# Cross-attention block on one core: the first nine steps and the last ones as lists of single-engine pieces

## The chip, the cores and the metric

The kernel runs on one core of one Trainium2 chip. The core has five engines with a queue of instructions each: PE (matmul; its weight loads are shown apart as PEld), DVE (vector), ACT (scalar and activation), POOL (GpSimd) and SP, which here only sends transfers. An engine works through its own queue in order and waits where an instruction needs another engine's result or a buffer that another still reads. The time is the device time in microseconds (us), the median of three runs.

## What is computed

A block of cross attention and a feed-forward net over x and ctx, both (128, 128, 256) in float32; 16 heads of 16, 1024 hidden units. Cut to what matters:

```python
q = (query @ Wq + bq).reshape(b, s, 16, 16).transpose(0, 2, 1, 3)   # k, v from ctx alike
scores = jnp.einsum('bhqd,bhkd->bhqk', q, k) / jnp.sqrt(16.0)
scores = jnp.where(j < i, scores, -1e30)          # a row sees the keys before it
attn = jax.nn.softmax(scores, axis=-1)
attn = attn.at[:, :, 0, :].set(0.0)
attn_out = einsum('bhqk,bhkd->bhqd', attn, v).transpose(0, 2, 1, 3).reshape(b, s, d) @ Wo + bo
x = layer_norm(query + attn_out, ln1_g, ln1_b)
ffn = jax.nn.relu(x @ W1 + b1) @ W2 + b2
out = layer_norm(x + ffn, ln2_g, ln2_b)
```

## The kernel before

The batch of 128 is done in 64 steps, p = 0 to 63, of two elements each. There is no scheduler: the order in which the program is written is the order in each engine's queue. Since the rows of a step are masked, its scores come in two halves: "hi" is the second half of the rows against all 128 keys (four PSUM banks, pss1_p_r), "lo" the first half against 64 keys (pss0_p_r).

One step goes as follows. The tokens get the bias of the output projection (`add_bo`, POOL, L265) and are transposed (`tokens`, DVE). PE projects keys, queries and values (`project`, `values`; pk, pq, pv), ACT copies them out as kT, qT and the two arrangements vz and vd of the values (L417, L427). PE makes the scores, DVE adds the mask (`mask`, L501) and takes the maximum (`maximum`), ACT the exponential, POOL the product with the reciprocal of the sums (`sums`, L540). The probabilities sm must then stand with keys on partitions: DVE transposes blocks of 32 (`turn`, L559, sm to tb) and 16 transfers (`bring`, L593, or `send` and `fetch` over memory) put the blocks at their places in pT. Steps 0 and 1 do it by PE instead (`turn_on_pe`, L608, into banks ptp, with a copy by ACT, L610). PE multiplies pT with the values (`weigh`, L625 and L635, pc), ACT copies that out (`context`, L647, cxT), PE makes the output projection (`attention_out`, L654, po), DVE adds the residual and takes statistics, ACT normalises (`norm1`), and x1 is transposed as x1T, by DVE and five transfers (`turn_x1`: x1t four times, then x1T). The net's two products are done by seven-product schemes in most steps (`Hidden`, L1155, with sums xS that POOL makes, and L1189 for the relus hT; `Second`, L1052, with sums hS by POOL, L1011 to L1017), in the first steps by plain products (`hidden`, L908; `second`). The second normalisation (`finish`, `norm2`, or the `_apart` forms with a bank pb) and `store` end the step, 2 to 5 steps after its scores.

PSUM has eight banks, b0 to b7, each a buffer that is rewritten only when its readers are done. In the first steps `bank()` deals out b4 to b7 in turn, by the order of the calls. Three arrays of 128 x 3072 a step (sm, tb, pT) share four wide buffers, in the order of the requests.

The steps are written in three ways. Steps 0 and 1 are inline (L1271 to L1333), steps 2 to 6 are functions (`third` L1352 to `sixth` L1529), steps 7 to 62 come from a table `order` of single pieces with a lag in steps (L1767), and the last step, with what is left of the ones ahead of it, is written out from L1807 on. In the first ways and the last, a call such as `maximum` or `sums` issues work on two or three engines at once.

Of the kernel before, what the change touches and what calls it, by code (L numbers as in the profile page):

```python
# [14 lines left out]
P = 128  # L15
# [5 lines left out]
def tile_cross_attention_block(  # L21
# [194 lines left out]
    turns = [0]  # L216

# [6 lines left out]

    def bank(name):
        turns[0] += 1
        return at_bank(4 + turns[0] % 4, name)
# [50 lines left out]
    def queries(p):  # L278
        st = states[p]
        st["qT"] = proj.tile([P, KC, TP], F32, tag="qT", name=f"qT_{p}")  # L280
        pq = project(wq, st["xT"], at_bank(4, f"pq_{p}") if p > 3 else bank(f"pq_{p}"))
        for m in range(KC):
            nc.scalar.activation(
                st["qT"][:, m, :], pq[:, m * TP : (m + 1) * TP], AF.Identity,
                bias=bqs_c[:, m : m + 1], scale=QSCALE,
            )
# [4 lines left out]
    def scale_wq():  # L291
        nc.scalar.activation(wq, wq, AF.Identity, bias=0.0, scale=QSCALE)
        nc.gpsimd.tensor_tensor(dq, bqs_c[:, 1:2], bqs_c[:, 0:1], ALU.subtract)

    def combine_wq():
# [83 lines left out]
    def keys(p):  # L379
        project_keys(p)  # L380
        copy_keys(p)

    def project_keys(p):
        st = states[p]
        st["kT"] = proj.tile([P, KC, 2, TP], F32, tag="kT", name=f"kT_{p}")
        st["pk"] = project(wk, st["cT"], at_bank(0, f"pk_{p}") if p > 3 else bank(f"pk_{p}"))

    def copy_keys(p, ms=range(KC), es=range(2)):
        st = states[p]
        pk = st["pk"]  # L390
        for m in ms:
# [15 lines left out]

    def values_out(p):
        spread_values(p)
        stack_values(p)  # L410
# [24 lines left out]

    def wide(name):
        return soft.tile([P, NS * (H + HH) * 32], F32, tag="wide", name=name, bufs=4)

    def room(p, hi):
# [4 lines left out]
        at = H * P if not hi else 0  # L444
        n = P if hi else HP
        st["sm", hi] = st["sm"][:, at : at + H * n].rearrange("p (h j) -> p h j", j=n)
        st["nmx", hi] = small.tile([P, H], F32, tag=f"nmx{hi}", name=f"nmx{hi}_{p}")

    def scores(p, hi):
# [18 lines left out]
        room(p, hi)  # L468

    def scores_both(p):  # L470

        st = states[p]
        for hi in range(2):
# [3 lines left out]
            room(p, hi)  # L477
        one, two = (0, 1), (2, 3)
# [17 lines left out]
    def mask(p, hi, rs):  # L496
# [3 lines left out]
        for r in rs:  # L500
            nc.vector.tensor_tensor(  # L501
                st["sm", hi][:, 4 * r : 4 * r + 4, :],
# [5 lines left out]
    def maximum(p, hi, part):  # L508
        st = states[p]
        n = P if hi else HP  # L510
        sm, nmx = st["sm", hi], st["nmx", hi]
        nc.vector.tensor_reduce(nmx[:, part], sm[:, part, :], AX.X, ALU.max, negate=True)
# [5 lines left out]
    def exponential(p, hi, part):  # L518
        sm = states[p]["sm", hi]
# [3 lines left out]

    def sums(p, hi, part):

        st = states[p]
        sm = st["sm", hi]
        n = sm.shape[2]
        rs = small.tile([P, H], F32, tag=f"rs{hi}", name=f"rs{hi}_{p}_{part.start}")
        if ("su", hi) in st:  # L530
            su, rs = st["su", hi][:, part], rs[:, part]
        else:
            su = small.tile([P, H], F32, tag=f"su{hi}", name=f"su{hi}_{p}_{part.start}")
            su, rs = su[:, part], rs[:, part]
            nc.vector.tensor_reduce(su, sm[:, part, :], AX.X, ALU.add)
        if ("rs", hi, part.start) in st:
            rs = st.pop(("rs", hi, part.start))
        else:
            nc.vector.reciprocal(rs, su)
# [4 lines left out]


# [7 lines left out]
    def turn(p, hi, t):  # L553

        st = states[p]
        if "tb" not in st:
# [4 lines left out]
            st["sm", hi].rearrange("p h j -> p (h j)")[:, t * 1024 : (t + 1) * 1024].rearrange(  # L561
# [35 lines left out]
    def turn_on_pe(p, hi, ts):  # L597

        st = states[p]
        sm = st["sm", hi].rearrange("p h j -> p (h j)")  # L600
# [3 lines left out]
        for t in ts:  # L604
            pt = bank(f"ptp{hi}_{p}_{t}")
            for i in range(4):
                at = (4 * t + i) * P
                nc.tensor.transpose(pt[:, i * P : (i + 1) * P], sm[:, at : at + P], ident)  # L608
            n = 4 * t if hi else H + 4 * t
            nc.scalar.copy(  # L610
                st["pT"][:, :, n : n + 4, :].rearrange("p i n a -> p n i a"),
                pt.rearrange("p (n i a) -> p n i a", i=NS, a=32),
            )
# [167 lines left out]
    def norm2_apart(p, at):  # L781
# [3 lines left out]
        ps = st["pb"] = at_bank(at, f"pb_{p}").rearrange("p (s d) -> p s d", s=2)  # L785
        for s in range(2):
# [4 lines left out]
    def finish_apart(p, parts=(0, 1)):  # L791
# [3 lines left out]
        if 1 in parts:  # L795
            nc.vector.tensor_tensor(t2, ps, be2_r[:, None, :].to_broadcast([P, 2, D]), ALU.add)
            store(p)
# [10 lines left out]
    def fold_norm1():  # L808


        ps = bank("ps_b1")
        n = DFF // NS
        for k in range(KC):
            for j in range(NS):
# [5 lines left out]
                )  # L820
        for j in range(NS):
            at = slice(32 * j, 32 * j + 1)
            nc.scalar.copy(b1s[at], ps[at, :n])
# [9 lines left out]
    def scale_w1():  # L833
        for k in range(KC):
# [4 lines left out]
    def fold_values():  # L839

        ps = bank("ps_bv")
# [5 lines left out]
        return ps  # L847

    def add_values(ps):
        nc.scalar.copy(bov_r, ps[:, :D])  # L850
# [29 lines left out]
    def turn_x1_on_pe(p):  # L880
        st = states[p]
        x1T = ffn.tile([P, NS, 4 * 32], F32, tag="x1T", name=f"x1T_{p}")
        st["x1T"] = x1T.rearrange("p i (s k a) -> p s i k a", s=2, k=KC)
        pt = transposed(st["x1"], f"ptn_{p}").rearrange(
            "p (k s i a) -> p k s i a", k=KC, s=2, i=NS
        )
        for k in range(KC):
            if p == 0:

                nc.scalar.activation(  # L890
                    st["x1T"][:, :, :, k, :], pt[:, k], AF.Identity,
                    bias=be1_c[:, k : k + 1], scale=g1_c[:, k : k + 1],
                )
            else:
                nc.scalar.copy(st["x1T"][:, :, :, k, :], pt[:, k])

    def hidden(p, fs, between=None, banks=(2, 3, 4, 0)):
        st = states[p]
        if fs[0] == 0:
            st["hT"] = ffn.tile([P, FC, TP], F32, tag="hT", name=f"hT_{p}", bufs=2)  # L900
        for f in fs[::2]:
            if p == 0:
                ph = bank(f"ph_{p}_{f}")
            else:
                ph = at_bank(banks[f // 2], f"ph_{p}_{f}")
            for i in range(2):
                for k in range(KC):
                    nc.tensor.matmul(  # L908
                        ph[:, i * TP : (i + 1) * TP].rearrange("p (s i a) -> p s i a", s=2, a=32),
                        w1[:, k, (f + i) * P : (f + i + 1) * P], st["x1T"][:, :, :, k, :],  # L910
                        start=(k == 0), stop=(k == KC - 1),
                    )
                    if p == 1:
                        empty(3 if f else 2)
            for i in range(2):
                nc.scalar.activation(
                    st["hT"][:, f + i, :], ph[:, i * TP : (i + 1) * TP], AF.Relu,
                    bias=(b1e_c if p else b1_c)[:, f + i : f + i + 1], scale=1.0,
                )
            if between:  # L920
                between(f)
# [23 lines left out]
    def mask_high(p, rs):  # L945
# [7 lines left out]
        for r in rs:  # L953
            nc.vector.tensor_reduce(
                st["nmx", 1][:, 4 * r : 4 * r + 4],
# [1099 lines left out]
```

## Time and profile before

| | us |
|---|---|
| median of three runs | 1487.75 (1486.59 to 1487.85) |
| the profiled execution's own time | 1487.3 |
| its span, first to last instruction | 1485.4 |
| PE busy | 1467.7 |
| POOL busy | 1390.1 |
| mean granted clock of PE | 0.999 |

How it is read: the span is what the trace covers, 1.9 us less than the execution's own time. Busy shares are means over stretches with different limits, so the windows, which give the busy time of each engine in a stretch, and the waits, which give what an engine waited for there, are needed beside them. In the rows of a trace, "out<-in" are the program's names for what is written and read, x is a count, and square brackets give the idle time before and what ended it. SPq and ACTq are the rows of transfers that SP and ACT send.

### The profile page before, as it was taken

To read this page: it belongs to the slowest core of one execution; us is meant where nothing else is said; L and a number is where in the kernel's file an instruction comes from. 1 tells how busy PE (TensorE), PEld (TensorE's weight loads), DVE (VectorE), ACT (ScalarE), POOL (GpSimd) and SP (SyncE) were. 2 spreads that over 40 slices of the span, in tenths; PEclk is the share of its full clock that TensorE was granted. 3 is DMA by queue.
4 is the path that set the end of the run, shared out by engine and by line. 5 is a ranking of instruction groups with operands and counts; after the bars stand their busy time and mean duration, and the time that the engine had idled before them with its cause. 6 is when DMAs were issued, how large, how long until landed. Compare 5 with 4: busy or idle time off the path is not lost.

```text
span 1485.4 us, 53956 instructions
## 1 busy us (share of the span) xinstructions
PE 1467.7 (99%) x19696; PEld 1380.1 (93%) x19696; DVE 1318.3 (89%) x2897; ACT 1323.7 (89%) x5279; POOL 1390.1 (94%) x1484
## 2 busy tenths in 40 slices
PE   8999999999999999999999999999999999999998
PEld 7788999999999999999999999999999999999988
DVE  7998899999999998999999989989989999999866
ACT  5657999999999999999999999999999999999863
POOL 6878899999999999999999999999999999999996
PEclk9999999999999999999999999999999999999999
DMA  8356556556666556566566566666565666564451
GB/s 202 84 112 146 137 137 144 140 140 143 148 138 150 137 136 154 141 138 143 143 135 160 138 136 141 144 140 153 139 142 134 147 141 151 139 146 120 113 163 57
DMA packets 417862, 206.20 MB, mean 139 GB/s; under 512 B 282432, under 2 KB 386112, under 8 KB 417600
## 3 DMA queue, kind: packets, MB, share of 16 engines
q1 hardware_dynamic: 415696, 201.70, 57.6%
q8 instruction: 158, 2.59, 0.8%
q10 hardware_dynamic: 1904, 1.06, 0.3%
q14 instruction: 104, 0.85, 0.2%
HBM read 71.84 MB, written 34.87 MB: 72 GB/s over the span
## 4 chain that ended last, share of the span: by engine, by line
PE 91%; POOL 3%; ACT 2%; DVE 2%; issue 1%; DMA 1%; POOLq 0%; ACTq 0%; DVEq 0%
PE phs L1155 25%; PE pX L1052 11%; PE py L1052 7%; PE pz L1052 7%; PE pv L403 7%; PE po L654 7%; PE pk L272 7%; PE pq L340 7%; PE pss L487 6%; PE pc L635 4%; PE pc L625 2%; ACT sm L985 1%; PE ph L908 1%; POOL sm L540 1%; PE pq L272 1%
## 5 line engine op out<-in xcount | busy, mean ns | idle before, releaser
L540 POOL TENSOR_TENSOR sm<-sm,rs 128x1024 f32<-128x1024 f32 x192 | 364.9, 1903 | 7.5 <-DVE rs L551 4.0
L985 ACT ACTIVATE sm<-pss,nmx 128x128 f32<-128x128 f32 x944 | 332.6, 399 | 8.0 <-issue 5.2
L985 ACT ACTIVATE sm<-sm,nmx 128x64 f32<-128x64 f32 x944 | 321.5, 360 | 2.4 <-DVE nmx L975 1.7
L1189 ACT ACTIVATE hT<-hT,b1e_c 128x256 f32<-128x256 f32 x480 | 216.0, 501 | 53.2 <-DVE hT L1180 53.2
L559 DVE STREAM_TRANSPOSE tb<-sm 128x1024 f32<-128x1024 f32 x186 | 227.3, 1225 | 1.3 <-POOL sm L540 1.1
L985 ACT ACTIVATION_READ_ACCUMULATOR sm<-pss,nmx 128x1 f32 x912 | 218.1, 239 | 0.0
L985 ACT ACTIVATION_READ_ACCUMULATOR sm<-sm,nmx 128x1 f32 x912 | 193.0, 212 | 0.0
L1155 PE MATMUL phs<-xS,w1t 128*128 128x128 f32 x1440 | 179.8, 275 | 0.7 <-POOL xS L1111 0.7
L1155 PEld LDWEIGHTS phs<-xS,w1t 128*128 128x128 f32 x1440 | 170.1, 192 | 0.9 <-POOL xS L1111 0.9
L968 DVE TENSOR_REDUCE nmx<-pss 128x4 f32<-128x512 f32 x224 | 152.8, 682 | 1.9
L393 ACT ACTIVATE kT<-pk,bkh,half 128x256 f32<-128x256 f32 x252 | 138.1, 557 | 4.1 <-PE pk L272 4.1
L501 DVE TENSOR_TENSOR sm<-pss,neg 128x256 f32<-128x256 f32 (+1 forms) x276 | 113.4, 437 | 17.8 <-PE pss L487 13.3
L1052 PE MATMUL pX<-wt,hS 128*128 128x128 f32 x960 | 127.1, 275 | 1.5 <-POOL hS L1015 1.3
L1155 PE MATMUL phs<-x1T,w 128*128 128x128 f32 x960 | 126.2, 275 | 1.0 <-DMA x1T<-x1t 0.8
L1155 PEld LDWEIGHTS phs<-x1T,w 128*128 128x128 f32 x960 | 120.7, 192 | 4.5 <-DMA x1T<-x1t 1.2
L654 PE MATMUL po<-wo,cxT 128*128 128x256 f32 x512 | 121.3, 380 | 0.8 <-ACT cxT L647 0.8
L403 PE MATMUL pv<-wv,cT 128*128 128x256 f32 x512 | 121.1, 379 | 0.0
L272 PE MATMUL pk<-cT,wk 128*128 128x256 f32 x504 | 119.4, 380 | 0.2 <-ACT sm L985 0.2
L1052 PEld LDWEIGHTS pX<-wt,hS 128*128 128x128 f32 x960 | 116.8, 192 | 1.9 <-POOL hS L1015 1.5
L403 PEld LDWEIGHTS pv<-wv,cT 128*128 128x128 f32 x512 | 97.1, 190 | 13.2
L654 PEld LDWEIGHTS po<-wo,cxT 128*128 128x128 f32 x512 | 92.7, 190 | 11.5 <-ACT cxT L647 1.4
L272 PEld LDWEIGHTS pk<-cT,wk 128*128 128x128 f32 x504 | 91.4, 190 | 10.7 <-ACT sm L985 0.4
(195 smaller groups left out, 4161.4 us busy)
## 6 DMA issues: line engine op xcount, KB each, us to landing
pT<-tb SPq DMA_DIRECT2D x968, 96.0 KB, 2.2
x1t<-tbx SPq DMA_DIRECT2D x252, 64.0 KB, 2.8
x1T<-x1t SPq DMA_DIRECT2D x63, 256.0 KB, 3.4
out_dram<-t SPq DMA_DIRECT2D x63, 256.0 KB, 4.4
xb<-in_x_dram SPq DMA_DIRECT2D x124, 128.0 KB, 3.2
cb<-in_ctx_dram SPq DMA_DIRECT2D x124, 128.0 KB, 3.4
x<-in_x_dram SPq DMA_DIRECT2D x31, 512.0 KB, 4.9
w<-in_L_xattn_W_dram SPq DMA_DIRECT2D x2, 1024.0 KB, 9.7
```

The lines of the kernel that those rows point to most:

```text
L272: nc.tensor.matmul(ps[:, m * TP : (m + 1) * TP], w[:, k, m * P : (m + 1) * P], src[:, k, :], start=(k == 0), stop=(k == KC - 1),)
L393: nc.scalar.activation(st["kT"][:, m, e, :], pk[:, m * TP : (m + 1) * TP], AF.Identity, bias=bkh[:, m, e : e + 1], scale=half[:, e : e + 1],)
L403: nc.tensor.matmul(pv[:, s * D : (s + 1) * D], st["cT"][:, k, s * P : (s + 1) * P], wv[:, k, :], start=(k == 0), stop=(k == KC - 1),)
L501: nc.vector.tensor_tensor(st["sm", hi][:, 4 * r : 4 * r + 4, :], st["sps", hi][r][:, : 4 * n].rearrange("p (n j) -> p n j", j=n), no[:, No ...
L540: nc.gpsimd.tensor_tensor(sm[:, part, :], sm[:, part, :], rs[:, :, None].to_broadcast([P, part.stop - part.start, n]), ALU.mult,)
L559: nc.vector.transpose(st["tb"][:, :, at : at + 256].rearrange("p j (n a) -> p n j a", a=32), st["sm", hi].rearrange("p h j -> p (h j)")[:, ...
L654: nc.tensor.matmul(po[:, s * D : (s + 1) * D], cxT[:, k, s, :], wo[:, k, :], start=(k == 0), stop=(k == KC - 1),)
L968: nc.vector.tensor_reduce(st["nmx", 1][:, 4 * r : 4 * r + 4], st["sps", 1][r].rearrange("p (n j) -> p n j", j=P), AX.X, ALU.max, negate=True,)
L985: nc.scalar.activation(sm[:, h, :], src, AF.Exp, bias=nmx[:, h : h + 1], scale=1.0, **({"accum_out": st["su", hi][:, h : h + 1]} if summed ...
L1052: nc.tensor.matmul(out, left(k), right(k), start=(first and k == 0), stop=(k == K - 1), skip_group_check=True,)
L1155: nc.tensor.matmul(ps[:, i * P : (i + 1) * P].rearrange("p (n a) -> p n a", a=32), left(i), right, start=(i == 0 and which not in self.ONT ...
L1189: nc.scalar.activation(self.hT[:, f], self.hT[:, f], AF.Relu, bias=b1e_c[:, f : f + 1], scale=1.0,)
```

## The change

The first nine slots (steps 0 to 8) and the last ones (from slot 61) are written as flat lists of pieces that use one engine each, in a newly chosen order. Between them the table's order stays, for slots 9 to 60. To that end the helpers are split: `maximum` (DVE) from `less` (POOL), `totals` and `reciprocal` (DVE) from `sums` (POOL), `turned` (PE) from `untile` (ACT), `project` from `keep_queries`, `x1_blocks` from `x1_untile`, `hidden` from `hidden_relu`; the last step's half into `last_products`, `last_sum`, `last_power`, `last_scale`, `last_shift` and `last_out`; `store` no longer stands in `finish_apart`. Banks of the first steps now come from a table by name (`HOMES`), wide buffers from a table `SOFT` for steps 0 to 6 and a rotation after that. Every instruction of before is there once, with its shape; the transfers of the second half of pT_2 are sent by SP, not by ACT.

```diff
     def bank(name):
-        turns[0] += 1
-        return at_bank(4 + turns[0] % 4, name)
+        return at_bank(HOMES[name], name)
...
     def wide(name):
-        return soft.tile([P, NS * (H + HH) * 32], F32, tag="wide", name=name, bufs=4)
+        kind, p = name.split("_")
+        turn_ = 3 * (int(p) - 7) + ("sm", "tb", "pT").index(kind)
+        at = SOFT[name] if name in SOFT else (2, 3, 1, 0)[turn_ % 4]
+        return soft.tile([P, NS * (H + HH) * 32], F32, tag=f"wide{at}", name=name)
...
+    def less(p, hi, part):
+        st = states[p]
         n = P if hi else HP
-        sm, nmx = st["sm", hi], st["nmx", hi]
-        nc.vector.tensor_reduce(nmx[:, part], sm[:, part, :], AX.X, ALU.max, negate=True)
+        sm, nmx = probabilities(p, hi), maxima(p, hi)
         nc.gpsimd.tensor_tensor(
...
     def steps(first, last):
...
+        for slot in range(first, last + 1):
+            for name, lag in order:
+                if 6 < slot - lag < NP - 1:
+                    ops[name](slot - lag)
...
-    turn_on_pe(0, 1, range(2))
-    add_values(ps_bv)
-    values_out(1)
-    turn_on_pe(0, 1, range(2, 4))
+    turned(0, 1, 0)
+    stack_values(1, (0,))
+    add_values()
...
-        hidden(0, range(3 * FC // 4, FC), lambda f: bring(p, nc.scalar, EVERY[8:]))
...
+    bring(2, nc.sync, EVERY[4:8])
+    bring(2, nc.sync, EVERY[12:16])
+    sums(3, 1, ONE)
+    bring(2, nc.sync, EVERY[8:12])
+    bring(2, nc.sync, EVERY[0:4])
...
-    steps(7, NP - 2)
+    steps(9, 60)
...
+    ops["relu0"](62)
+    context(61)
+    ops["n2b"](62)
...
+    last_sum(0)
+    last_products(1)
+    finish_apart(62, (0,))
+    finish_apart(61, (1,))
+    finish_apart(62, (1,))
+    store(61)
+    last_sum(1)
+    store(62)
+    store(58)
+    last_scale(0)
+    store(60)
+    store(59)
+    last_power(0)
+    last_scale(1)
+    last_shift(0)
+    last_power(1)
+    last_out(0)
+    last_shift(1)
+    last_out(1)
```

Three places show how the order moves. The first is ACT's queue where steps 0 and 1 meet: ptp are the transposed probabilities of step 0 (hi 0_0 to 0_3 and lo), pv the values of step 1. Before:

```order
L393 ACTIVATE kT_1_338<-pk_1_339,bkh_216,half_167 128x256 x4
L520 ACTIVATE sm_0_263<-sm_0_263 128x1024
L610 COPY pT_0_394<-ptp1_0_0_395 128x4x4x32
L610 COPY pT_0_394<-ptp1_0_1_401 128x4x4x32
L850 COPY bov_r_184<-ps_bv_359 128x256
L417 COPY vz1_178<-pv_1_354 128x8x2x16 x2
L427 COPY vd1_180<-pv_1_354 64x16x16 x2
L610 COPY pT_0_394<-ptp1_0_2_412 128x4x4x32
L610 COPY pT_0_394<-ptp1_0_3_418 128x4x4x32
```

And after:

```order
L421 COPY vz1_178<-pv_1_332 128x8x2x16
L540 ACTIVATE sm_0_273<-sm_0_273 128x1024
L431 COPY vd1_180<-pv_1_332 64x16x16
L867 COPY bov_r_184<-ps_bv_379 128x256
L431 COPY vd1_180<-pv_1_332 64x16x16
L627 COPY pT_0_402<-ptp1_0_0_383 128x4x4x32
L421 COPY vz1_178<-pv_1_332 128x8x2x16
L627 COPY pT_0_402<-ptp1_0_1_397 128x4x4x32
L627 COPY pT_0_402<-ptp1_0_3_416 128x4x4x32
```

Three of the four copies of pv_1 now stand ahead of the first pT copy, the last behind it. In both kernels ptp1_0_2 takes pv_1's bank.

The second place is ACT's queue where the last steps begin: hT_59 are the relus of step 59, cxT the context of step 61, which PE's next output projection reads. Before:

```order
L427 COPY vd0_176<-pv_62_22322 64x16x16
L1189 ACTIVATE hT_59_22328<-hT_59_22328,b1e_c_187 128x256
L770 ACTIVATE t2_57_21812<-t2_57_21812,nb_62_22359,sd_62_22358 128x256
L417 COPY vz0_174<-pv_62_22322 128x8x2x16
L1189 ACTIVATE hT_59_22328<-hT_59_22328,b1e_c_187 128x256 x7
L647 COPY cxT_182<-pc_61_22510 128x4x127
```

And after:

```order
L787 ACTIVATE t2_57_21643<-t2_57_21643,nb_62_21933,sd_62_21932 128x256
L421 COPY vz0_174<-pv_62_22101 128x8x2x16
L1190 ACTIVATE hT_59_22128<-hT_59_22128,b1e_c_187 128x256
L664 COPY cxT_182<-pc_61_22290 128x4x127
L787 ACTIVATE t2_57_21643<-t2_57_21643,nb_62_21933,sd_62_21932 128x256
L1190 ACTIVATE hT_59_22128<-hT_59_22128,b1e_c_187 128x256 x7
```

The copy to cxT moves ahead of seven relus and one half of a normalisation.

The third place is the end of DVE's queue: py_last_0 and _1 are the last step's two halves, pb_61 and pb_62 the second normalisations of steps 61 and 62. Before:

```order
L2009 TENSOR_TENSOR py_last_0_23367<-py_last_0_23367,t2_63_23251 128x256
L2011 BN_STATS bs_last_0_23377<-py_last_0_23367 128x6
L2012 BN_AGGR mv_last_23365<-bs_last_0_23377 128x2
L2015 SCALAR_TENSOR_TENSOR py_last_0_23367<-py_last_0_23367,mv_last_23365,g2_r_151 128x256
L794 TENSOR_TENSOR pb_62_23362<-pb_62_23362,g2_r_151 128x512
L796 TENSOR_TENSOR t2_62_23062<-pb_62_23362,be2_r_153 128x512
L2018 SCALAR_TENSOR_TENSOR t2_63_23251<-py_last_0_23367,sd_last_23366,be2_r_153 128x256
L2009 TENSOR_TENSOR py_last_1_23388<-py_last_1_23388,t2_63_23251 128x256
L2011 BN_STATS bs_last_1_23398<-py_last_1_23388 128x6
L2012 BN_AGGR mv_last_23365<-bs_last_1_23398 128x2
L2015 SCALAR_TENSOR_TENSOR py_last_1_23388<-py_last_1_23388,mv_last_23365,g2_r_151 128x256
L2018 SCALAR_TENSOR_TENSOR t2_63_23251<-py_last_1_23388,sd_last_23366,be2_r_153 128x256
```

And after:

```order
L1542 BN_AGGR mv_last_23191<-bs_last_0_23194 128x2
L811 TENSOR_TENSOR pb_62_23188<-pb_62_23188,g2_r_151 128x512
L813 TENSOR_TENSOR t2_61_22779<-pb_61_23148,be2_r_153 128x512
L813 TENSOR_TENSOR t2_62_22966<-pb_62_23188,be2_r_153 128x512
L1539 TENSOR_TENSOR py_last_1_23197<-py_last_1_23197,t2_63_23063 128x256
L1541 BN_STATS bs_last_1_23211<-py_last_1_23197 128x6
L1542 BN_AGGR mv_last_23191<-bs_last_1_23211 128x2
L1553 SCALAR_TENSOR_TENSOR py_last_0_23179<-py_last_0_23179,mv_last_23191,g2_r_151 128x256
L1553 SCALAR_TENSOR_TENSOR py_last_1_23197<-py_last_1_23197,mv_last_23191,g2_r_151 128x256
L1559 SCALAR_TENSOR_TENSOR t2_63_23063<-py_last_0_23179,sd_last_23192,be2_r_153 128x256
L1559 SCALAR_TENSOR_TENSOR t2_63_23063<-py_last_1_23197,sd_last_23192,be2_r_153 128x256
```

The scaling and the shift of the first half move behind the second half's statistics, and a piece of step 61 (pb_61) comes in between. On SP the five stores of steps 58 to 62 stand last in both kernels, ahead of the two of step 63; their order was 58, 60, 59, 61, 62 and is now 61, 62, 58, 60, 59. Step 61's store is then ready when its piece on DVE, shown above, is done.

More of the change, by code (lines that the diff above doesn't have):

```diff
@@ L898, in hidden, with hidden_relu @@
+    def hidden_relu(p, f):
         st = states[p]
-        if fs[0] == 0:
+        if "hT" not in st:
             st["hT"] = ffn.tile([P, FC, TP], F32, tag="hT", name=f"hT_{p}", bufs=2)
[L901 to L921, printed above, removed]
+        g = f // 2 * 2
+        nc.scalar.activation(
+            st["hT"][:, f, :], st["ph", g][:, (f - g) * TP : (f - g + 1) * TP], AF.Relu,
+            bias=(b1e_c if p else b1_c)[:, f : f + 1], scale=1.0,
+        )
@@ L1788, in step_tables @@
         return ops, order
+    ops, order = step_tables()
     def steps(first, last):
[L1791 to L1804 removed]
@@ new lines, in tile_cross_attention_block @@
+    less(3, 1, ONE)
+    mask(3, 1, (2,))
+    residual1(0, nc.gpsimd, (1,))
+    scores(3, 0)
+    maximum(3, 1, TWO)
+    second(0, 1)
+    norm1(1, (0,))
+    nc.gpsimd.tensor_tensor(b1e_c, b1e_c, b1_c, ALU.add)
+    less(3, 1, TWO)
+    block_x1(1)
+    mask(3, 0, (0,))
+    stack_values(3, (0,))
+    exponential(3, 1, ONE)
+    mask(3, 0, (2,))
+    scale_w1((0,))
+    mask(3, 0, (3,))
+    tokens(6, "x")
+    spread_values(3, (1,))
+    scale_w1((1,))
+    mask(3, 0, (1,))
+    maximum(3, 0, ALL)
@@ new lines, in tile_cross_attention_block @@
+    add_bo(63)
+    both_shifts(*later)
+    residual1(61, nc.gpsimd, (0,))
+    w60 = Second(60, banks=(1, 6, 4))
+    w60.run(2)
+    w60.run(4)
+    w60.run(1)
+    h61.run(4)
+    w60.run(5)
+    leave_x1(62)
+    fetch_x1(62)
+    w60.add(0)
+    w60.run(6)
+    h61.add5()
+    h61.add4()
+    w60.add(2)
+    w60.add(1)
+    h61.run(3)
+    weigh(63)
+    residual1(61, nc.gpsimd, (1,))
+    h61.add3()
+    w60.run(7)
+    combine_normed(62, (2,))
+    h61.relu(2)
+    combine_normed(62, (0,))
```

2015 lines of the change are left out of this document (1421 added, 594 removed), and 9 rows, old and new, of the table HOMES.

## The prediction

> **What bounds the kernel now.** I read the page first: the span, the engines' busy shares and the chain that ended last.
>
> ```profile
> span 1485.4 us, 53956 instructions
> PE 1467.7 (99%) x19696; PEld 1380.1 (93%) x19696; DVE 1318.3 (89%) x2897; ACT 1323.7 (89%) x5279; POOL 1390.1 (94%) x1484
> PE 91%; POOL 3%; ACT 2%; DVE 2%; issue 1%; DMA 1%; POOLq 0%; ACTq 0%; DVEq 0%
> ```
>
> PE is busy for 99% of the span, and 91% of the chain is its own work, so the matmuls set the time. The change keeps every matmul and every shape, and can only win time in which PE stands still or runs slowly. Where that is, the windows view tells: each row is a stretch, its length, the busy time of PE, PEld, DVE, ACT and POOL, the granted clock, the DMA share and GB/s.
>
> ```profile
> 20.00:30.00 10.00, 7.35 (x89) 5.52 (x95) 9.02 (x13) 7.21 (x16) 9.87 (x6) 0.88 0.95 270
> 40.00:172.00 132.00, 128.13 (x1575) 108.43 (x1556) 116.21 (x201) 93.08 (x274) 108.52 (x100) 1.00 0.52 118
> 172.00:1403.00 1231.00, 1231.00 (x16889) 1174.64 (x16887) 1119.12 (x2523) 1166.12 (x4833) 1187.48 (x1261) 1.00 0.60 141
> 1403.00:1486.00 83.00, 72.82 (x867) 68.26 (x865) 53.99 (x125) 42.11 (x133) 66.73 (x86) 0.99 0.39 109
> ...
> 24.00:28.00 4.00, 1.78 (x15) 1.58 (x14) 3.93 (x7) 3.09 (x9) 4.00 (x3) 0.96 1.12 347
> 28.00:31.00 3.00, 3.00 (x59) 2.34 (x61) 1.94 (x3) 2.50 (x4) 2.87 (x3) 0.50 0.69 110
> ```
>
> From 172 to 1403 us PE never stops. That stretch is steps 9 to 60, whose order is kept, so nothing is to be won there. The stops are at the two ends: 10.00 − 7.35 = 2.65 us in 20:30, 132.00 − 128.13 = 3.87 in 40:172, and 83.00 − 72.82 = 10.18 in the last stretch. There is also a slow piece: in 28:31 the clock is 0.50, so 3 us of PE time do 1.5 us of work, and in 24:28 it is 0.96, another 0.2: 1.7 us in all. The waits of PE name the releasers (total, times, longest), first for 0:172, then for 1403:1486; for 172:1403 the view is empty.
>
> ```profile
> PE ptp L608 <- issue: 2.2, 1, 2.2
> PE warm L1210 <- POOL ident masks.py:199: 1.5, 1, 1.5
> PE po L654 <- ACT cxT L647: 0.8, 1, 0.8
> PE pss L487 <- ACT hT L916: 0.8, 2, 0.6
> PE ph L908 <- ACT kT L393: 0.8, 1, 0.8
> PE phs L1155 <- POOL xS L1111: 0.7, 1, 0.7
> ...
> PE ph L908 <- DMA x1T<-x1t: 0.2, 1, 0.2
> ...
> PE pss L487 <- ACT cxT L647: 1.5, 1, 1.5
> PE pX L1052 <- POOL hS L1015: 1.3, 1, 1.3
> PE phs L1155 <- DMA x1T<-x1t: 0.8, 1, 0.8
> ```
>
> The end after the last matmul is the third place; here are PE's last work, DVE's and SP's last rows (start, duration, engine, line, operation).
>
> ```profile
> 1472.92 7.07 PE L2005 MATMUL py_last<-w,hT 128*128 128x256 f32 x32
> ...
> 1480.96 0.18 DVE L2012 BATCH_NORM_AGGREGATE mv_last<-bs_last 128x2 f32<-128x6 f32 x1
> 1481.18 0.49 DVE L2015 SCALAR_TENSOR_TENSOR py_last<-py_last,mv_last,g_r 128x256 f32<-128x256 f32 x1
> 1482.07 0.48 DVE L2018 SCALAR_TENSOR_TENSOR t<-py_last,sd_last,be_r 128x256 f32<-128x256 f32 x1 [0.40 <-POOL sd_last L2014]
> ...
> 1480.06 2.88 SPq L2019 DMA_DIRECT2D out_dram<-t  x2
> ```
>
> PE ends at 1472.92 + 7.07 = 1479.99. Of the 10.18 us in the last stretch 6.01 thus lie behind it, and 4.17 are waits. So at most 2.65 + 3.87 + 1.7 + 4.17 = 12.4 us can go ahead of the last matmul: a floor of 1487.3 − 12.4 = 1474.9 us for the profiled execution, 0.8% below it. A time that moves by less than 0.2% (3 us) I count as unchanged; that is about what a measurement of this kernel can tell.
>
> **The change part by part.** All sums are made against the profiled execution's own 1487.3 us (its span of 1485.4 and 1.9 around it), 0.45 below the median of 1487.75.
>
> *T1, the first bank wait.*
>
> ```profile
> 23.44 1.09 PE L608 MATMUL ptp<-ident,sm 128*128 128x128 f32 x8 [0.43 <-POOL sm L540]
> 26.75 1.51 PE L608 MATMUL ptp<-ident,sm 128*128 128x128 f32 x10 [2.22 <-issue]
> ...
> 24.13 1.07 ACT L610 COPY pT<-ptp 128x512 f32<-128x512 f32 x2 [1.51 <-PE ptp L608]
> 25.35 0.68 ACT L417 COPY vz<-pv 128x256 f32<-128x256 f32 x2
> 25.88 0.76 ACT L427 COPY vd<-pv 64x256 f32<-64x256 f32 x2
> ...
> 21.48 5.62 POOL L540 TENSOR_TENSOR sm<-sm,rs 128x1024 f32<-128x1024 f32 x3
> ...
> 24.07 1.22 DVE L501 TENSOR_TENSOR sm<-pss,neg 128x512 f32<-128x512 f32 x2
> ```
>
> The view says "issue", yet what PE waits for is the bank: the third transposed piece goes where pv_1 lies until ACT's four copies of it end at 26.64, and those stand behind two pT copies that wait for PE. After the change three of the four stand ahead of the first pT copy, one behind it: 24.13 + 0.55 for that copy + 0.35 for the last one and 0.1 to release give 25.1 instead of 26.75. The stop is 0.5 then. PE's 8 transposes from there take 0.9, to 26.0. Next it now does the low scores of step 1, whose banks DVE frees with four masks, at 24.07 + 4 × 0.61 = 26.5: a second stop of 0.6. The low transposes behind need POOL's third product, which ends at 21.48 + 5.62 = 27.10; the scores (0.6) cover that. With the 0.43 ahead of the first transposes, which POOL's product still sets (POOL is full here, 9.87 of 10), some 1.5 to 2.1 of the 2.65 are left: **−0.8** (bounds 0 and −2.2; I take the middle of what POOL's and DVE's rows allow).
>
> *T2, the slow clock.* The half clock comes right behind the 2.22 us stop. With that stop split into pieces of 0.4 to 0.6, no stretch is left in which PE is as empty as the 1.78 of 4.00 us of 24:28. The tail has a stop of 1.5 and one of 1.3 us, and its clock stays at 0.99 over 83 us. The new pieces are nearer to these than to 2.22: **−1.7** (bounds 0 and −1.7). [...]
>
> *T3, steps 2 to 8.* Here are 3.87 us of stops, 3.5 of them named above: ACT copies that stand behind an exponential or a relu (0.8, 0.8, 0.8), POOL's sums and small ones. The new lists put cxT, kT and the relus ahead of long ACT pieces and xS ahead of POOL's projections. Against this stands the SP queue: all 16 transfers of pT_2 go out there, where 8 went by ACT's.
>
> ```profile
> 58.73 1.22 DVE L559 STREAM_TRANSPOSE tb<-sm 128x1024 f32<-128x1024 f32 x1
> ...
> 62.46 4.46 ACTq L593 DMA_DIRECT2D pT<-tb  x7
> 64.03 5.99 SPq L593 DMA_DIRECT2D pT<-tb  x8
> ...
> 71.81 0.34 PE L625 MATMUL pc<-pT,vd 128*32 128x64 f32 x11
> ...
> pT<-tb SPq DMA_DIRECT2D x968, 96.0 KB, 2.2
> x1T<-x1t SPq DMA_DIRECT2D x63, 256.0 KB, 3.4
> ```
>
> Transfers start when tb's last third is done, now at 59.95. DVE then no longer has a residual between the thirds (0.6 earlier), and the step as a whole is 2.5 us ahead by T1 and T2: 56.9. Sixteen at 0.67 us (4.46 / 7 = 0.64, 5.99 / 8 = 0.75) take 10.7, and 2.2 to land: 69.8. PE wants pT_2 at 71.81 − 2.5 = 69.3, so it waits some 0.5 us; were the cover gone, it would be up to 8 × 0.67 = 5.4. I allow 0.7 more for the same in x1T_3 and pT_5, which stand behind transfers waiting for DVE. So 1.2 of the 3.87 stay: **−2.7** (bounds −3.9, and +2.2 with 5.4 in the place of 0.5). The banks and wide buffers of the tables are as many as before (4 and 4); I cost the new assignment at nothing beside T1, as PE's work between two uses of a bank is some us and covers the copy of 0.55.
>
> *T4, the last steps.* ACT and POOL in 1403:1412:
>
> ```profile
> 1404.32 2.90 ACT L1189 ACTIVATE hT<-hT,b1e_c 128x256 f32<-128x256 f32 x7
> 1411.73 1.27 POOL L1011 TENSOR_TENSOR hS<-hT 128x512 f32<-128x512 f32 x1
> ```
>
> cxT of step 61 stood behind these seven relus; now it stands ahead of six or seven of them, up to 2.8 us earlier, and the wait of 1.5 goes. The relus end 1.1 later (a copy of 0.56 and a normalising of 0.59), at 1408.3. POOL's first hS_59 stood behind seven 128x512 pieces; of these only three stand between the last product and it now, so it starts when the relus are done, some 3 us earlier, and the wait of 1.3 goes too. The x1T of step 61 is sent earlier, but still behind a pT block: I count 0.3 of its 0.8. Together **−3.1** (bounds 0 and −4.2).
>
> *T5, behind the last matmul.* DVE now does both last scalings after the second statistics, then both shifts: from 1481.14 four pieces at about 0.47 to 1483.0, where the last shift ended at 1482.55: +0.5. Three finishing pieces of 0.69 stand between the two halves' statistics and just fit before PE's end. And the five stores of 256 KB of steps 58 to 62, spread over 20 us before, are issued in the last 4, ahead of the two last ones: 1.3 MB at the 347 GB/s that 24:28 shows is 3.8 us from about 1479.8, done at 1483.6, while the last shift is sent at 1483.1; at the 109 GB/s of the last stretch it would be 12.0, done at 1491.8 where the span now ends at 1485.4. I take the first, being the stretch with many transfers queued at once, and 0.5 for sharing: **+1.0** (bounds +0.5 and +6.4).
>
> Sum: −0.8 − 1.7 − 2.7 − 3.1 + 1.0 = −7.3, so 1487.3 − 7.3 = 1480.0 for a profiled run and, with 0.45 to the median, **1480.5 us**.
>
> **The rivals.**
>
> [...]
>
> *The lead is not kept.* POOL is at 1187.48 of 1231.00 us in the steady stretch, 96%. If POOL, not PE, is ahead by less than the 5.2 us of T1 to T3, PE meets it again and waits at the first steps of the steady order; then only T4 and T5 remain, −2.1: 1485.6 (1487.75 − 2.1). For it: POOL's share. Against it: its slack of 43 us there, and POOL's own queue had gaps ahead of 172 (108.52 of 132 busy) that go with the reordering.
>
> *Slower: SP's queue as the bound of steps 2 to 8.* A step sends 16 pT, 4 x1t, one x1T and the loads through one queue; a transfer that waits for DVE holds all behind it, and PE wants x1T and pT at about the time when they land. If in each of these seven steps PE waits one landing (2.2 us) for it, it is 15.4 us: 1480.5 + 15.4 = 1495.9. It decides for slower from (7.3 + 3.0) / 7 = 1.5 us a step. For it: pT_2 comes out with no slack. Against it: 40:172 has a DMA share of 0.52, and only 0.2 us of a stop there is put down to a DMA now.
>
> *The order doesn't set the engines.* If what the new lists move is not what the waits hang on, every stop returns elsewhere: 1487.75, at most the end's +1.0.
>
> **How the numbers follow.** Forecast 0.60 (1476 to 1484), clock 0.14 (1482.2), lead lost 0.10 (1485.6), no effect 0.06 (1488), slower 0.10 (1496). The bounds 1484.8 and 1490.7 are 0.2% around the median. Faster: 0.60 + 0.14 + 0.01 from the lower side of the lead's loss = 0.75. Same: 0.09 + 0.06 = 0.15. Slower: 0.10. The range leaves out the slower case and the lower end of the sum's bounds (0.05): it goes from 1476.0, 1.1 above the floor, to 1488.5.
>
> **What would show it.** T1: ptp's second start near 25.1, after a stop of under 1 us. T2: 0.50 nowhere in 24:34. T3: PE busy over 130 of 132 in 40:172, and one stop at pc of step 2. T4: no stop over 0.5 us for cxT or hS behind 1395. T5: the time from PE's last end to the span's end 6.4 instead of 5.4 us. The forecast is wrong if PE has stops after 172, if SP's queue releases over 3 us of them ahead of it, or if the span behind the last matmul exceeds 9 us.

## The result and the profile after

| | before | after |
|---|---|---|
| median of four runs (us) | 1487.80 (1486.59 to 1488.63) | 1479.53 (1479.12 to 1480.06) |
| ratio, 95% interval | | 0.9945 (0.9928 to 0.9962) |
| profiled execution, its span (us) | 1487.3, 1485.4 | 1480.06, 1478.1 |

The changed kernel is 0.55% faster: 8.3 us by the medians, 7.3 by the two spans. Among the later runs two single executions, one of e_tail (7027.65 us) and one of b_copies (1509.18), lie far off the others of their kernels and do not enter the ratios. First the page of the changed kernel: span, engines, chain.

```profile
span 1478.1 us, 53969 instructions
PE 1464.9 (99%) x19696; PEld 1378.9 (93%) x19696; DVE 1316.4 (89%) x2897; ACT 1325.7 (90%) x5279; POOL 1389.8 (94%) x1484
PE 94%; POOL 1%; DVE 1%; DMA 1%; SPq 1%; issue 1%; ACT 0%; DVEq 0%; POOLq 0%
```

PE's share of the chain rises from 91 to 94%; the shares of POOL and ACT fall. The windows (length, busy time of PE, PEld, DVE, ACT, POOL, clock, DMA share, GB/s), with the stretch of steps 9 to 60 seven us earlier than before:

```profile
20.00:30.00 10.00, 8.99 (x116) 6.07 (x118) 9.90 (x17) 7.02 (x15) 10.00 (x6) 1.00 0.90 266
40.00:172.00 132.00, 130.41 (x1580) 113.77 (x1577) 119.45 (x210) 98.64 (x302) 113.86 (x107) 1.00 0.56 125
165.00:1396.00 1231.00, 1230.59 (x16880) 1174.01 (x16879) 1118.80 (x2522) 1164.66 (x4829) 1185.84 (x1260) 1.00 0.60 141
1396.00:1479.00 83.00, 73.61 (x876) 69.39 (x874) 54.41 (x126) 44.58 (x139) 67.24 (x87) 0.97 0.38 109
24.00:28.00 4.00, 3.25 (x55) 2.67 (x53) 3.96 (x8) 2.60 (x7) 4.00 (x3) 1.00 1.11 355
28.00:31.00 3.00, 3.00 (x94) 2.51 (x96) 3.00 (x7) 2.31 (x5) 3.00 (x3) 1.00 0.89 144
```

In 20:30 PE stands still for 1.01 us where it was 2.65, and the clock of 28:31 is 1.00 where it was 0.50. (The 0.97 of the 1396:1479 row comes from the 7 us behind PE's last work: 0.68 in 1472:1479, 1.00 in 1396:1472.) PE's waits, for 0:165, 165:1396 and 1396:1479:

```profile
PE pc L642 <- DMA pT<-tb: 1.1, 1, 1.1
PE ptp L619 <- POOL sm L557: 0.7, 1, 0.7
PE pc L642 <- DMA x1t<-tbx: 0.4, 1, 0.4
PE pss L476 <- ACT qT L294: 0.3, 1, 0.3
...
PE po L671 <- issue: 0.4, 1, 0.4
...
PE phs L1156 <- DMA x1T<-x1t: 1.9, 2, 1.6
PE pX L1064 <- POOL hS L1027: 0.2, 1, 0.2
```

The waits for ACT's copies (cxT, kT, hT) are gone from the first steps. What ends last there now are transfers, 1.1 and 0.4, the second at the products of step 2, and POOL's product, 0.7. In the last steps cxT is gone and hS is at 0.2, but a stop of 1.6 for x1T of step 60 is new. The end, from the timeline:

```profile
1469.84 1.89 PE L1528 MATMUL py_last<-w,hT 128*128 128x256 f32 x8
1471.04 2.73 SPq L816 DMA_DIRECT2D out_dram<-t  x5
1473.56 0.87 DVE L1559 SCALAR_TENSOR_TENSOR t<-py_last,sd_last,be_r 128x256 f32<-128x256 f32 x2
1474.06 1.19 SPq L1564 DMA_DIRECT2D out_dram<-t  x2
```

PE ends at 1471.73, and 6.4 us follow where 5.4 did. DVE's last shift ends at 1474.43, 2.7 us behind PE, where it was 2.6 (1482.55 − 1479.99), so nearly all of the 1.0 lies in the transfers: the five stores are sent in 2.73 us, right ahead of the two last ones.

To tell the first steps' share from that of the last, I read one landmark in each trace: the start of the same output projection in the steady stretch (that of step 58), and, at the head, of the scores of step 2. First the rows of before, then those of after.

```profile
39.36 0.90 PE L459 MATMUL pss<-kT,qT 32*64 32x256 f32 x24
...
1339.62 1.89 PE L654 MATMUL po<-wo,cxT 128*128 128x256 f32 x8
```

```profile
36.68 1.12 PE L476 MATMUL pss<-kT,qT 32*64 32x256 f32 x32
...
1333.66 1.89 PE L671 MATMUL po<-wo,cxT 128*128 128x256 f32 x8
```

At step 2's scores PE is 2.7 us ahead, in the steady stretch 6.0. The last matmul ends 8.3 ahead (1479.99 to 1471.73), so the last steps give 2.3; then 1.0 is lost behind it: 6.0 + 2.3 − 1.0 = 7.3.

### The profile page after: what moved, and what is told of

The parts are those of the page before. It is cut to its first block, busy times and chain, and to the rows that moved or that the text cites. A ratio compares the mean times of both kernels' runs of the same rounds, so it can differ in the third digit from the quotient of the medians.

```text
span 1478.1 us, 53969 instructions
## 1 busy us (share of the span) xinstructions
PE 1464.9 (99%) x19696; PEld 1378.9 (93%) x19696; DVE 1316.4 (89%) x2897; ACT 1325.7 (90%) x5279; POOL 1389.8 (94%) x1484
## 3 DMA queue, kind: packets, MB, share of 16 engines
q8 instruction: 158, 2.59, 0.8%
## 4 chain that ended last, share of the span: by engine, by line
PE 94%; POOL 1%; DVE 1%; DMA 1%; SPq 1%; issue 1%; ACT 0%; DVEq 0%; POOLq 0%
PE phs L1156 25%; PE pX L1064 11%; PE pk L281 7%; PE py L1064 7%; PE po L671 7%; PE pz L1064 7%; PE pv L411 7%; PE pq L351 7%; PE pss L502 6%; PE pc L652 4%; PE pc L642 2%; PE ph L917 1%; SPq L608 1%; DMA x1T<-x1t 1%; POOL sm L557 1%
## 5 line engine op out<-in xcount | busy, mean ns | idle before, releaser
L980 DVE TENSOR_REDUCE nmx<-pss 128x4 f32<-128x512 f32 x236 | 160.8, 683 | 1.9
```

Source lines behind the costliest of these rows:

```text
L980: nc.vector.tensor_reduce(maxima(p, 1)[:, 4 * r : 4 * r + 4], st["sps", 1][r].rearrange("p (n j) -> p n j", j=P), AX.X, ALU.max, negate=True,)
```

## The experiments

The table gives for each kernel the median, the ratio to the runs of before on its chip with its interval, and from its trace the lead of PE at that landmark against the first trace of before (late is positive), the further change of the last steps up to the last matmul, and the time behind it.

| kernel | median | ratio | lead, step 58 | last steps | behind |
|---|---|---|---|---|---|
| changed, first trace | 1479.53 | 0.9945 (0.9928–0.9962) | −6.0 | −2.3 | 6.4 |
| a_again | 1479.56 | 0.9950 (0.9938–0.9963) | −7.0 | −2.3 | 6.4 |
| e_head | 1479.70 | 0.9947 (0.9935–0.9959) | −7.8 | −0.4 | 5.4 |
| e_head2 | 1480.47 | 0.9954 (0.9942–0.9967) | −6.8 | −0.1 | 5.4 |
| e_tail | 1485.31 | 0.9986 (0.9977–0.9994) | −1.3 | −2.2 | 6.4 |
| b_copies | 1488.17 | 1.0003 (0.9994–1.0011) | −0.2 | −0.4 | 5.4 |
| b_fill | 1494.90 | 1.0046 (1.0033–1.0059) | +9.2 | −0.2 | 5.4 |
| b_shift | 1498.87 | 1.0079 (1.0065–1.0092) | +13.0 | +0.4 | 5.4 |
| b_ctx | 1487.51 | 1.0001 (0.9992–1.0009) | 0.0 | −0.2 | 5.4 |
| a_act | 1485.33 | 0.9984 (0.9975–0.9993) | −1.9 | −2.0 | 6.4 |
| a_end | 1480.37 | 0.9948 (0.9936–0.9960) | −7.2 | −0.1 | 5.4 |
| a_x1 | 1483.45 | 0.9968 (0.9956–0.9981) | −6.1 | 0.0 | 6.4 |
| a_best | 1477.41 | 0.9934 (0.9922–0.9946) | −6.6 | −3.4 | 5.4 |

### e_tail and e_head: one end of the program at a time

e_tail has the first steps (and the rules for banks and wide buffers) of before and the new list from slot 61 on; e_head the reverse.

```diff
-    scores(0, 1)
-    first_tokens(1, "c")
...
-    steps(9, 60)
+    third()
+    fourth()
+    fifth()
+    fall_in(5)
+    sixth(6)
+    steps(6, 60)
```

> The first nine steps in the order of before, the last steps in the new order. If the gain is the sum of separate places: the stops of the last steps shrink by about 2.3 us, the time behind the last matmul grows by about 1.0, so 1486.5 us against 1487.8 (-1.3). If the last steps gain only because the first ones hand them a lead: no change or slower, 1487.8 to 1489.

> The first nine steps in the new order, the last ones in the order of before. If the lead of the first steps is carried through the steady stretch: about -6.0 us, 1481.8. If POOL, or the steady order, takes the lead back and the gain sits in the last steps: 1486 to 1488, with stops of PE behind 172 us.

Both gain, so neither end hangs on the other. The lead of the first steps arrives unshortened at the landmark, and the last steps shrink by 2.2 us, pay 1.0 at the end, with or without that lead. Of e_tail's gain 1.3 us are not the last steps': its trace is that much ahead at the landmark, with the first steps of before, because its clock in 28:31 is 1.00 (see b_fill and b_shift). POOL does not take the lead back: the stretch 165:1396 has 1231.00 us of PE's work in e_head. e_head did better than its 1481.8: its lead was 7.8, not 6.0.

### a_again and e_head2: the changed kernel again, and beside it

> The changed kernel itself once more, as the measure for the two next ones: 1479.5 us within 1 us. If the 0.85 us by which PE's lead shrinks at slots 9 to 10 in its first trace belongs to the kernel, it is there again; if it is an accident of one execution, the lead in the steady stretch is larger this time (-6.8 or more against the kernel before).

> The first nine steps in the new order, the last ones in the order of before, beside the changed kernel on one chip. If the new order of the last steps adds something on top of the new first steps (its stops 2.3 us shorter, its end 1.0 us longer): about 1.3 us slower than the changed kernel, 1480.8. If it adds nothing on top: equal.

The second trace of the changed kernel has a lead of 7.0: the 0.85 us that the first one lost between the output projections of steps 8 and 9 belongs to that execution. Beside each other, the new last steps are worth 1480.47 − 1479.56 = 0.9 us, near the 1.3 expected; the two intervals overlap, so the runs alone don't show it, the traces (2.2 less stops, 1.0 more end) do.

### b_copies: only the first stop

```diff
-    turn_on_pe(0, 1, range(2))
     add_values(ps_bv)
     values_out(1)
+    turn_on_pe(0, 1, range(2))
```

> The kernel before with one thing moved: ACT's copy of the folded bias and its four copies of pv_1 stand ahead of the first two pT copies instead of behind them. If the first stop is the wait for pv_1's bank, it falls from 2.2 us to about 0.7; if the half clock comes from that stop, the clock is 1.00 in 28 to 31 us as well: -1.5 - 1.2 to 1.7, about -2.9 us in all (1484.9). [...]

A miss: no gain, although the stop did go (2.2 us for the bank before; 0.8 and 0.8 for POOL's product now) and the clock was 1.00. The scores of step 2 began 2.15 us earlier, at 37.21. Most of that is the clock: against e_tail, whose clock is 1.00 too and whose first stop is that of before, they begin 0.6 earlier (37.78 to 37.21). Then, at the products of step 2, the trace of this kernel has a stop that the kernel before does not have:

```profile
72.43 0.43 PE L625 MATMUL pc<-pT,vd 128*32 128x64 f32 x16 [2.92 <-DMA pT<-tb]
...
61.95 0.39 SPq L100 DMA_DIRECT2D x<-in_x_dram  x1
62.63 8.11 SPq L593 DMA_DIRECT2D pT<-tb  x8
```

SP sends its half of pT_2 from 62.63 to 70.74, in 8.11 us where the kernel before takes 5.99, and PE waits for it until 72.43. The earlier start by itself is not the cause. Right ahead of the eight stands a load of x, 512 KB, which the kernel before sends at 53.45. SP's waits for that load, first before, then in b_copies:

```profile
SPq L100 <- DMA xb<-in_x_dram: 1.1, 1, 1.1
...
SPq L100 <- DMA pT<-tb: 11.8, 1, 11.8
```

Here the load waits 11.8 us, until ACT's first transfer of pT_2 has landed at 61.89. In this kernel's trace the two carry the same semaphore number, 105; in the kernel before, the load shares its number, 104, with a transfer of xb that lands at 53.39. So moving ACT's copies also moved a load in among the transfers of pT_2, and those landed later: the median of ACT's eight is 3.7 us, where it was 2.4. That a lead can pass this place shows in e_tail, which comes to the products of step 2 at 70.17, 1.55 us ahead of the kernel before (71.72), without a stop there. The changed kernel sends all sixteen from 56.79 on, in 11.51 us, and there the stop is 0.4. What the first stop alone is worth at the end of the kernel is therefore not shown by this run.

### a_act: half of pT_2 by ACT's queue again

```diff
-    bring(2, nc.sync, EVERY[12:16])
+    bring(2, nc.scalar, EVERY[12:16])
...
-    bring(2, nc.sync, EVERY[8:12])
+    bring(2, nc.scalar, EVERY[8:12])
```

> The changed kernel with half of pT_2's transfers on ACT's queue again. If one queue for all sixteen costs PE the wait of 0.4 us at the products of step 2, that wait goes (-0.4 at most). If instead ACT, which is held about 5 us by sending them, delays its exponentials of step 3, the lead of the first steps shrinks: +0.5 to +3 us, with new stops of PE between 70 and 110 us.

5.8 us slower than the changed kernel, more than either theory gave. ACT comes to these transfers late, behind its exponentials:

```profile
72.90 0.32 PE L642 MATMUL pc<-pT,vd 128*32 128x64 f32 x8 [3.37 <-DMA pT<-tb]
...
65.68 1.23 ACTq L608 DMA_DIRECT2D pT<-tb  x2
```

SP's half is out by 61.6, ACT's begins at 65.68, and PE stops for 3.4 us; in the 3.5 us behind the stop the clock is 0.61, which adds to the loss. So in the new order, at this place of ACT's queue, the eight transfers cost most of the first steps' gain, and sending them by SP, which I had put down as a risk, saves it. An earlier place on ACT, such as the kernel before has (from 61.82 on), was not tried.

### b_fill and b_shift: the clock, and something else

b_fill gives PE work in the first stop; b_shift puts as many empty instructions (28) at the same place.

```diff
     turn_on_pe(0, 1, range(2))
+    fill = at_bank(4 + (turns[0] - 1) % 4, "fill")
+    for i in range(14):
+        at = i % 4 * P
+        nc.tensor.transpose(
+            fill[:, at : at + P],
+            states[0]["sm", 1].rearrange("p h j -> p (h j)")[:, at : at + P], ident,
+        )
     add_values(ps_bv)
```

```diff
     turn_on_pe(0, 1, range(2))
+    empty(28)
     add_values(ps_bv)
```

> The kernel before with 14 more transposes on PE (about 1.6 us of work whose result nobody reads) put into the first stop; no wait is shortened. If the clock follows how busy PE was, it stays at 1.00 in 28 to 31 us and the kernel gets 1.2 to 1.7 us faster (1486.3) although it does more work. If the clock does not depend on it, 0.50 stays and the time is the same or up to 0.3 longer.

> The kernel before with 28 empty instructions on PE's queue at the place where b_fill had its 14 transposes (28 instructions), no other work. b_fill lost 7 us mostly in steps 9 to 60, at places where PE waited for nothing that the profile shows. If that comes from where PE's instruction stream is cut into fetched blocks, the same shift by 28 gives the same loss: about 1494 us. If the filler's work itself was the cause: 1487.8, as before.

Both are far slower, b_shift without any added work and by 4 us more than expected (1498.87 against about 1494). The waits of b_shift, in all and, for the second row, at the first stop; then its steady stretch:

```profile
PE pq L340 <- issue: 7.0, 18, 0.4
PE ptp L608 <- ACT vd L427: 2.2, 1, 2.2
...
165.00:1396.00 1231.00, 1223.75 (x16902) 1163.50 (x16906) 1108.19 (x2492) 1154.75 (x4764) 1174.78 (x1249) 1.00 0.60 140
```

In 18 steps of the steady stretch PE now stops for 0.4 us at the query products, released by nothing that the profile shows, where the kernel before has no stop at all. Nothing differs in that stretch but the count of instructions ahead of it on PE's queue, 28 more; its transfers carry the semaphore numbers of before. That these 28 cost 11.9 us in this run (1498.87 against 1486.97) is measured; why they do was not shown. The pages list transfers of instructions (q8: 158 packets, 2.59 MB in the kernel before); that they make the stops is not shown either, and it was not tried by itself. 7 of the 13 us are in these waits, the rest is spread too thin to read.

The second row also names what the first trace had called "issue": the first stop is ACT's copies of pv_1, as the prediction read it.

The clock itself shows in two kernels that have the old first steps and the same stop of 2.2 us. The row 28:31 of e_tail, then that of b_ctx:

```profile
28.00:31.00 3.00, 3.00 (x134) 2.41 (x133) 2.97 (x7) 2.31 (x5) 2.87 (x3) 1.00 0.77 127
```

```profile
28.00:31.00 3.00, 3.00 (x72) 2.34 (x74) 1.68 (x3) 2.46 (x4) 2.87 (x3) 0.58 1.03 159
```

Behind the same stop the clock falls in one execution and not in another: 28:31 has 1.00 in e_tail, 0.58 in b_ctx and 0.50 in the kernel before; in b_shift the slow piece began earlier (0.69 in 24:28, 0.84 in 28:31). In the eight traces with the new first steps it did not come: 24:28 and 28:31 have 1.00 in each.

Behind two longer stops of later steps it came as well: 0.61 in the 3.5 us behind a_act's stop of 3.4, and 0.62 in 1420:1424 of a_x1, whose stop of 3.8 ends at 1419.72. In b_copies, with stops of 0.8 and 0.8 and PE busy for 2.47 of the 4.00 us of 24:28, the clock is 1.00. In b_fill, where the filler leaves 0.51 us of the stop (0.24 and 0.27) and PE is busy for 3.49 of the 4.00 us, it is 1.00 too, as it should be if the clock follows how busy PE was. But e_tail also has 1.00, with PE busy for only 1.78 of the 4.00 us, as in the kernel before (1.78) and b_ctx (1.78). So that the filler kept the clock up is not shown, and its time was lost elsewhere. What decides between e_tail's case and the other two was not shown either.

### b_ctx: cxT alone in the last steps

```diff
+                if p <= last or name in ("weigh", "ctx"):
...
-    weigh(p - 2)
-    context(p - 2)
```

> The kernel before with one thing moved: ACT's copy of the context of step 61 stands at the table's place, ahead of five relus of step 59, instead of behind all of them. If the 1.5 us stop at 1406 is that copy, it goes and PE's later work comes 1.5 earlier, of which the wait for hS_59 on POOL (1.3 now) can take back all, since hS_59 waits for relus that now end 0.55 later: between -1.5 and 0 us, I expect about -0.3 with the hS wait grown to about 2.5. If both stops go by this alone: -2.5.

As expected: the stop of 1.5 for cxT went and nothing was won. PE came earlier to the sums of hidden units, which POOL still made as late. The waits of b_ctx:

```profile
PE py L1052 <- POOL hS L1011: 1.7, 1, 1.7
...
PE pX L1052 <- POOL hS L1015: 1.3, 1, 1.3
```

The new list also has only three of POOL's 128x512 pieces between the product and hS_59, where seven stood. Both moves together shorten the stops (2.2 us in e_tail); the second alone was not run.

### a_x1, a_end and a_best: what the change left

a_x1 sends x1T_60 earlier and the store of step 56 later; a_end places each store where its data is ready and gives DVE the old order for the two last halves; a_best has the end of a_end, and x1T_60 early with the store right behind it. The first diff is a_best's; in a_x1 the store line stands behind `ops["br4"](62)` instead. The second is the end of both a_end and a_best.

```diff
     ops["turn2"](62)
-    ops["br0"](62)
-    ops["store"](61)
+    bring(62, nc.sync, EVERY[0:3])
     ops["x1in"](62)
+    ops["store"](61)
+    bring(62, nc.sync, EVERY[3:4])
```

```diff
     finish_apart(60, (1,))
+    store(60)
...
     finish(58, (1,))
+    store(58)
...
     finish(59, (1,))
+    store(59)
+    finish_apart(61, (1,))
+    store(61)
     last_products(0)
...
     last_sum(0)
+    last_power(0)
+    last_scale(0)
     last_products(1)
     finish_apart(62, (0,))
-    finish_apart(61, (1,))
     finish_apart(62, (1,))
-    store(61)
+    store(62)
+    last_shift(0)
+    last_out(0)
     last_sum(1)
...
```

> The changed kernel with SP's order changed at one place: x1T of step 60 goes out behind three instead of four transfers of pT_62 and ahead of the store of step 56. If SP's queue is what makes PE wait 1.6 us for x1T_60, x1T goes out about 1.4 us earlier and the stop falls to about 0.2: -1.4, 1478.1, unless the stop at x1T_61 (0.35 now) grows by the same, then 0. If the landing of x1t, not the queue, holds it: 0.

The stop at x1T_60 went as SP's queue theory had it, and the kernel got 3.9 us slower for a reason that neither theory held:

```profile
1414.57 1.30 POOL L761 TENSOR_TENSOR t<-t,g_r 128x512 f32<-128x512 f32 x1 [4.36 <-DMA out_dram<-t]
...
1419.72 2.05 PE L1156 MATMUL phs<-xS,w 128*128 128x128 f32 x8 [3.78 <-DVE hT L1178]
```

POOL's residual of step 60 writes the buffer that the store of step 56 reads. With the store sent 9 us later, POOL waited 4.4 us for it, DVE for POOL, PE for DVE.

> The changed kernel with the end rewritten: each store of steps 58 to 62 stands where its data is ready, and DVE has the order of before for the last step's two halves. If the bunch of stores (1.6 MB at about 340 GB/s, 4.6 us) sets the end, the time behind the last matmul falls from 6.4 to about 5.3 us: -1.1, 1478.4. If DVE's and POOL's last pieces set it alone: -0.2 to -0.4.

The end did shrink by 1.0 (from 6.4 to 5.4 us), and with DVE's share at 0.1 that is the bunch of stores. But in this trace PE's stops for x1T of steps 60 to 62 were longer, and the median is no better than the changed kernel's:

```profile
PE phs L1156 <- DMA x1T<-x1t: 4.0, 3, 1.7
```

SP's order up to there is the same in both. Step 62's x1T, for one, could go out 5.2 us after its first x1t (1430.30 to 1435.50), where the changed kernel's took 4.3 (1432.14 to 1436.46); why the landing took longer is open.

> The changed kernel with the end of a_end, and with x1T of step 60 sent behind three instead of four transfers of pT_62 but the store of step 56 kept right behind it, so that its buffer comes free as early as now. If a_x1 lost its time only to the late store: the stop at x1T_60 goes (-1.4) and the end is 1.0 shorter, 1477.1 us. If an earlier x1T_60 only moves the stop to x1T_61 and x1T_62: 1478.5.

1477.41, 2.15 us below the changed kernel on the same chip, and 0.66% below the kernel before; its lowest and highest runs (1477.18 and 1477.94) lie below every run of the changed kernel. Its waits and its last work on PE:

```profile
PE phs L1156 <- DMA x1T<-x1t: 0.7, 1, 0.7
...
1462.99 7.07 PE L1528 MATMUL py_last<-w,hT 128*128 128x256 f32 x32
```

x1T stops PE once, for 0.7, and 5.4 us follow the last matmul.

## Why the prediction was right, and where it was not

The time forecast was 1480.5 us; 1479.53 was measured, and the profiled run moved by the forecast 7.3. That the sum agrees to the tenth is luck: the terms are off by −0.6, +0.4, −0.6 and +0.8, which cancel, and the second trace moved by 8.3. The terms:

| term | forecast | measured | from |
|---|---|---|---|
| T1, bank wait | −0.8 | −1.4 | the rest of the 2.7 |
| T2, clock | −1.7 | −1.3 in this pair | 12.61 to 11.35, below |
| T1 and T2 by step 2's scores | −2.5 | −2.7 | 39.36 to 36.68 |
| T3, steps 2 to 8 | −2.7 | −3.3; −4.2 in a_again | 6.0 − 2.7; 7.0 − 2.8 |
| T4, last steps | −3.1 | −2.3 | 8.3 − 6.0 |
| T5, behind PE | +1.0 | +1.0 | 5.4 to 6.4 |

**T1.** The mechanism holds, and b_shift's trace names ACT's copies. In the changed kernel's timeline the third piece starts here (PE, ACT's last copy of pv_1, POOL's three products):

```profile
25.39 1.06 PE L619 MATMUL ptp<-ident,sm 128*128 128x128 f32 x8 [0.75 <-POOL sm L557]
...
24.92 0.38 ACT L421 COPY vz<-pv 128x256 f32<-128x256 f32 x1
...
21.38 5.62 POOL L557 TENSOR_TENSOR sm<-sm,rs 128x1024 f32<-128x1024 f32 x3
```

It starts at 25.39 (25.1 forecast) after 0.75 (0.5 forecast). The view names POOL, whose second product ends near 25.1, but ACT's copy ends later, at 25.30: the bank is still the last to come. The stops in 20:30 fell by 1.6 (2.65 to 1.01), of which 1.4 arrive at step 2's scores. The second stop forecast, 0.6 for DVE's masks ahead of the scores, did not come, and that is the 0.6 by which the term was too small. That T1 counts by itself to the end is not shown, since in b_copies a load that moved with it took the lead back.

**T2.** I took the half clock as what this stop does, and its price as 1.7. Its price shows against e_tail, which has the same first steps at full clock:

```profile
26.43 1.94 PE L621 MATMUL ptp<-ident,sm 128*128 128x128 f32 x16 [2.21 <-issue]
...
37.78 1.12 PE L478 MATMUL pss<-kT,qT 32*64 32x256 f32 x32
```

From there to step 2's scores e_tail takes 11.35 us, the kernel before 12.61 (26.75 to 39.36): 1.3. And the lead of 1.6 that e_tail has at the first output projection (0.3 of it from its start) is still 1.3 at step 58, so this term does count by itself. The half clock came behind this stop in some executions: 28:31 has 0.50 in the kernel before and 0.58 in b_ctx, b_shift an earlier piece (0.69 in 24:28), e_tail 1.00. What decides was not shown. Part of T2 is therefore luck of the profiled run, though the shorter stops have not brought it in 24 to 31 us in eight traces, where PE is busy for 3.25 or 3.26 of the 4.00 us of 24:28 (behind the later stops of 3.4 us in a_act and 3.8 in a_x1 it was 0.61 and 0.62).

**T3.** The right sign and a size too small: I had counted visible stops only, 3.87 (the lines named add to 3.3, not 3.5), and the lead grew by 3.3 here and by up to 4.7 in a_end. What is gained beyond the stops is open. The landings named as tight were the ones that came up: 0.4 at the products of step 2 (0.5 forecast), and 1.1 at those of step 5, for which, with x1T_3, 0.7 was allowed. What I had costed as a risk of the eight moved transfers is shown by a_act to be a gain in this order: with half of them on ACT at the same place, PE waits 3.4 us.

**T4.** cxT's and hS's stops went as worked out (b_ctx shows that moving cxT alone wins nothing). The step that failed is the 0.3 won at x1T, where 1.1 was lost. The 1.6 us at x1T_60 was not in the forecast: PE now comes to it earlier, while it stands on SP behind four transfers of pT_62 and a store. a_best takes most of it back.

**T5.** Right in sum; DVE's part is 0.1 instead of 0.5, the stores' 0.9 instead of 0.5.

**The rivals.** That POOL would take the lead back is refuted by e_head. By its own signs the forecast would be wrong if PE stopped after 172; the first trace has one such stop, 0.41 at 212.24, put down to "issue". a_again and e_head have none, so it belongs to that execution. That the stops would still halve the clock (0.14, for 1482.2: the sum without T2) did not come true: 24:28 and 28:31 have 1.00 in eight traces. That SP's queue would bound steps 2 to 8 has its mechanism in the traces (1.1 and 0.4 us of stops), far below the 1.5 us a step from which it would have decided.

## What to carry to other kernels

Where one engine is busy all the time, the gain of an earlier start lasts only until the next thing it waits for: before moving one wait, look up what its successor will wait for. b_ctx removed its stop and met POOL's sums; b_copies removed its own and met a transfer that a load, sent later than before, had delayed. After a reordering, compare the transfers too, not only the engine that was reordered. A store that nobody waits for can still hold a buffer: a_x1 lost 4 us on POOL because a store was sent later. And compare several traces before giving a change the credit for a clock that one execution happened to show: behind the same stop of 2.2 us it was 0.50 in the kernel before and 1.00 in e_tail.

## What the runs showed that was not expected

28 empty instructions on PE's queue, at a place where PE waits anyway, cost 11.9 us (1498.87 against 1486.97), among others through stops of 0.4 us in 18 later steps, for which the profile shows no releaser.
